# Range checks of a two-layer attention kernel: pieces of 128x256 in place of 128x512

## The chip, the core and the metric

The kernel runs on one core of a Trainium2 chip, which has 8 of them. A core has five engines that run side by side and wait for each other through semaphores: TensorE (PE, matrix products; its weight loads are listed as PEld), VectorE (DVE), ScalarE (ACT), GpSimd (POOL) and SyncE (SP), whose queue here issues most of the transfers. The engines work on a memory on the chip, SBUF, with 128 partitions; matmuls write to a second one, PSUM. A tile named 128x512 has 128 partitions and 512 float32 numbers in each.

The metric is the time of one execution on the device, in microseconds (us), the median of several runs. A profile is taken in a separate execution, in which every instruction is recorded; its time is a little different and is given beside its span.

## What is computed

An input of 128 x 256 x 256 (T, F, C) goes through two layers, each of which normalises by groups of channels (`_gn`), applies an attention along F for each of the 128 rows, and adds the result to its input. Layer 0 has 8 heads, a gate and an additive bias made from a second input `z`; layer 1 has 4 heads, and a query sees only keys at most 16 places away. Cut to what matters:

```python
# layer 0
scores = jnp.einsum('bsihc,bsjhc->bshij', q, k) * scale + b
mask2d = msa_mask[..., :, None] * msa_mask[..., None, :] > 0
scores = jnp.where(mask2d[:, :, None], scores, NEG_INF)
p = jax.nn.softmax(scores, axis=-1)
o = jnp.einsum('bshij,bsjhc->bsihc', p, v).reshape(B, s, i, h * c) * gate
x = x + (o @ Wo.T + bo)
# layer 1, on the result of layer 0
qkv = _gn(x).reshape(B * T, F, C) @ w_in.T + b_in
scores = jnp.einsum('bhid,bhjd->bhij', q, k) / jnp.sqrt(D)
scores = jnp.where(jnp.abs(i - j) <= band, scores, -jnp.inf)
attn = jax.nn.softmax(scores, axis=-1)
out = jnp.einsum('bhij,bhjd->bhid', attn, v)
x = x + (out @ w_out.T + b_out)
```

## The kernel before

The program holds two versions of the computation. `fast_kernel` leaves out what a softmax needs for extreme values (it takes exponentials without subtracting a maximum, and leaves out the mask), and checks as it goes that the numbers were in a range where this is right. `general_kernel` runs after it only where a check failed (`mixer_kernel`, L2067). With the inputs here it doesn't run.

A check is three VectorE instructions, in the helper `check` (L954 to 961): L958 compares the tile with a lower bound and writes 1 or 0 into a scratch tile `chk`; L959 compares with an upper bound and multiplies with `chk`; L960 takes the minimum along the row and writes it into one column of the tile `ok`. `chk` has one buffer of 128x512. At the end, L2060 takes the minimum over the columns of `ok`, and a small matmul brings the 128 rows together to the verdict.

Layer 1 works on pairs of rows: 64 pairs (`NP`), p = 0 to 63, in one loop from L1998. The order is written out by hand (`manual_schedule`), so every engine's instructions stand in the order in which the loop's lines issue them. An iteration finishes pair p-1 (`was`), does most of pair p (`now`) and prepares p+1, p+2 and p+3 (`nxt`, `nn`, `n3`). The parts that the prediction's steps touch, in the order of the loop:

- `now.scores(r)`: products of keys and queries (L1874, PE), their exponential (L1883, ACT), and the multiplication with the band's pattern `bw` (L1885, POOL, two instructions of 128x384).
- `was.apply(1)`: products with the values and the sums (L1903, PE).
- `nxt.product(n, i)`: seven products for queries (n = 0) and keys (n = 1) with the weights mixed in a fast scheme (L1824, PE), in the order 1, 2, 6, 5, 7, 4, 3. Each tile of PSUM is used twice over: `nxt.join(n, 2)` (L1835, VectorE) reads the result of product 2 and writes it into `qT` or `kT`, and product 5 then starts anew in the same PSUM tile. So product 5 waits for the join of product 2.
- `was.invert(1)`: the sums and their reciprocals (L1921, L1922, VectorE); `was.weigh(1)`: L1926, L1928 (VectorE).
- `was.out_row(r)`: the output projection (L1943, PE), and the addition of the input (L1947, VectorE).
- `nxt.values(r)`: L1860 (PE) and a copy (L1864, ACT).
- `nn.centre`, `nn.differences()`: L1786 (ACT), L1788 and L1795 to L1798 (POOL).
- `n3.turn()`: a transpose of 128x1024 on VectorE (L1781), one in each iteration up to p = 60.
- Then, as the last thing of an iteration with p > 0, one check from the list `checks`, if there is one (L2039). On VectorE it stands behind the transpose and ahead of the next iteration's joins for product 2.

The list `checks` is filled by `check_all` (L1964), one entry for each piece of 512 columns: the table `eb` (128x4096, 8 pieces), the mask (128x256, 1 piece), and the sums of layer 0 (`sums0`, 128x2048, 4 pieces). They go to iterations 1 to 13. In iteration 58, `load_sums` (L2004) fetches the sums of layer 1's first 56 pairs (`sums1`, 128x896) and adds pieces of 512 and 384 columns, which go to iterations 58 and 59. The last 8 pairs' reciprocals `rv` are checked directly in `weigh` (L1933, L1935), not through the list.

Of the kernel before, what the change touches and what calls it, by code (L numbers as in the profile page):

```python
# [9 lines left out]
F32 = mybir.dt.float32  # L10
# [6 lines left out]
P = 128  # L17
# [756 lines left out]
def fast_kernel(  # L774
# [41 lines left out]
    const = ctx.enter_context(tc.tile_pool(name="const", bufs=1))  # L816
# [114 lines left out]
    for a in range(KC):  # L931
        for h in range(H1):
            n = P // H1
# [5 lines left out]
    for h in range(H1):  # L939
        n = P // H1  # L940
# [7 lines left out]
    kb = const.tile([P, KC], F32, name="kb")  # L948
    vb_r = const.tile([P, C], F32, name="vb_r")
    bz_r = const.tile([P, H], F32, name="bz_r")  # L950
    ok = const.tile([P, 32], F32, name="ok")
    done = []

    def check(src, lo, hi, pool):  # L954

        n = src.shape[1]
        a = pool.tile([P, 512], F32, name="chk", tag="chk", bufs=1)[:, :n]
        nc.vector.tensor_scalar(a, src, lo, None, ALU.is_gt)  # L958
        nc.vector.scalar_tensor_tensor(a, src, hi, a, ALU.is_lt, ALU.mult)  # L959
        nc.vector.tensor_reduce(ok[:, len(done) : len(done) + 1], a, AX.X, ALU.min)  # L960
        done.append(src)
# [601 lines left out]
    behind, nx, n = None, 0, 0  # L1563
# [140 lines left out]
    with tc.tile_pool(name="l1", bufs=2) as sb, tc.tile_pool(  # L1704
        name="l1s", bufs=4
    ) as sm, tc.tile_pool(name="ps1_s", bufs=4, space=PSUM) as ps_s, tc.tile_pool(
        name="ps1_o", bufs=1, space=PSUM
# [254 lines left out]
        checks = []  # L1962

        def check_all(src, lo, hi):  # L1964
            for i in range(0, src.shape[1], 512):
                n = min(512, src.shape[1] - i)
                checks.append(lambda i=i, n=n: check(src[:, i : i + n], lo, hi, sm))

        def load_sums(src, name):
            t = sb.tile([P, src.shape[0] // P], F32, name=name, tag=name, bufs=1)  # L1970
            nc.sync.dma_start(t, src.rearrange("(a b) -> a b", a=P))
            check_all(t, 1e-16, 1e8)

        with tc.manual_schedule():
# [12 lines left out]
            for k in range(KC):  # L1987
                nxt.centre(k)
            nxt.differences()
        check_all(eb.rearrange("p h b i -> p (h b i)"), math.exp(-20.0), math.exp(20.0))  # L1990
        mask_t = sb.tile([S, I], F32, name="mask_all", bufs=1)
        nc.sync.dma_start(mask_t, mask)
        check_all(mask_t, 1e-15, 1e15)
        load_sums(rsum.rearrange("n q r c i -> (n q r c i)"), "sums0")

# [70 lines left out]
@with_exitstack  # L2066
def mixer_kernel(ctx, tc, *args):  # L2067

    nc = tc.nc
    keep = ctx.enter_context(tc.tile_pool(name="verdict", bufs=1))  # L2070
    verdict = keep.tile([1, 1], mybir.dt.int32, name="verdict")
    fast_kernel(tc, *args, verdict)
    again = nc.values_load(verdict[0:1, 0:1], min_val=0, max_val=1)
    with tc.If(again > 0):
        general_kernel(tc, *args)
# [53 lines left out]
```

## Time and profile before

| | us |
|---|---|
| median of 3 runs (3231.11 to 3235.41) | 3231.37 |
| the profiled execution | 3251.55 |
| its span, first to last instruction | 3249.8 |
| of it: layer 0 and what comes ahead of it (to about 2040) | 2040 |
| layer 1's beginning, to the transpose of its first iteration with a check | 83.4 |
| 13 intervals with a check of the list (2123.36 to 2362.70) | 239.3 |
| 42 intervals without a check (2362.70 to 3110.39) | 747.7 |
| the rest: pairs with checks of `rv` and `sums1`, and the end | 139.4 |

An interval is the time from one transpose (L1781) to the next, one iteration long. The page gives for each engine its busy time and its share of the span: PE 3073.5 us (95%), DVE 2339.4 (72%), POOL 2157.6 (66%), ACT 1537.5 (47%). These are means over stages that have different limits, so a change to one stage is read in that stage's own rows. In a timeline row stand the start, the length, the engine, the line, the operation, the tiles out<-in with their sizes, and in brackets how long the engine stood idle before it, with what ended the idling.

### The profile page before, as it was taken

To read this page: it belongs to the slowest core of one execution; us is meant where nothing else is said; L and a number is where in the kernel's file an instruction comes from. 1 tells how busy PE (TensorE), PEld (TensorE's weight loads), DVE (VectorE), ACT (ScalarE), POOL (GpSimd) and SP (SyncE) were. 2 spreads that over 40 slices of the span, in tenths; PEclk is the share of its full clock that TensorE was granted. 3 is DMA by queue.
4 is the path that set the end of the run, shared out by engine and by line. 5 is a ranking of instruction groups with operands and counts; after the bars stand their busy time and mean duration, and the time that the engine had idled before them with its cause. 6 is when DMAs were issued, how large, how long until landed. Compare 5 with 4: busy or idle time off the path is not lost.

```text
span 3249.8 us, 82756 instructions
## 1 busy us (share of the span) xinstructions
PE 3073.5 (95%) x34916; PEld 2066.9 (64%) x34916; DVE 2339.4 (72%) x3684; ACT 1537.5 (47%) x2501; POOL 2157.6 (66%) x1631
## 2 busy tenths in 40 slices
PE   5379999999999999999999999699999999999998
PEld 3245555555555555555555555488888888888886
DVE  7966676777777777777777777577766666666676
ACT  2255444444444444444444444255555555555553
POOL 3368888888888887888788886355454555545453
PEclk9799999999999999999999999899999999999999
DMA  9953333434433442344343332533334334343431
GB/s 349 391 150 63 65 88 86 95 70 96 95 95 70 95 91 64 87 92 95 70 95 96 67 88 70 106 80 89 92 88 92 91 90 95 85 100 86 94 93 47
DMA packets 726973, 329.10 MB, mean 101 GB/s; under 512 B 574560, under 2 KB 675808, under 8 KB 725440
## 3 DMA queue, kind: packets, MB, share of 16 engines
q1 hardware_dynamic: 721520, 320.81, 40.3%
q8 instruction: 277, 4.54, 0.7%
q10 hardware_dynamic: 5072, 2.90, 0.3%
q14 instruction: 104, 0.85, 0.1%
HBM read 254.88 MB, written 68.75 MB: 100 GB/s over the span
## 4 chain that ended last, share of the span: by engine, by line
PE 71%; DMA 12%; DVE 8%; POOL 4%; issue 2%; ACT 1%; SPq 1%; ACTq 0%; DVEq 0%; POOLq 0%
PE ps_p L1322 13%; PE ps_qk L1824 11%; PE ps_v L1860 7%; PE ps_su_y L1943 7%; PE ps_sc L1356 6%; PE ps_y L1443 5%; PE ps_ov L1388 5%; PE ps_v L1337 5%; PE ps_o L1903 3%; DMA rvb<-rsum 3%; PE ps_sc L1874 3%; DMA rs_d<-lrs 3%; DMA rsum<-rv 3%; PE ps_su L1396 2%; POOL eboth L1377 2%
## 5 line engine op out<-in xcount | busy, mean ns | idle before, releaser
L1377 POOL TENSOR_TENSOR eboth<-e 128x512 f32<-128x512 f32 x512 | 639.4, 1272 | 214.8 <-DVE e L1372 214.7
L1363 ACT ACTIVATE ps_sc<-ps_sc 128x1024 f32<-128x1024 f32 x512 | 492.8, 1006 | 575.9 <-PE ps_sc L1356 575.9
L1372 DVE TENSOR_TENSOR e<-ps_sc,eb 128x1024 f32<-128x1024 f32 x512 | 602.9, 1219 | 221.8 <-ACT ps_sc L1363 219.2
L1885 POOL TENSOR_TENSOR e<-e,bw 128x384 f32<-128x384 f32 x256 | 252.7, 1008 | 520.3 <-ACT e L1883 520.3
L1356 PE MATMUL ps_sc<-qT,kT 32*128 32x256 f32 x4096 | 293.3, 400 | 2.0 <-ACT kT L1326 2.0
L1443 PEld LDWEIGHTS ps_y<-wo,oT 128*128 128x128 f32 x1024 | 190.8, 190 | 106.6 <-POOL oT L1433 51.1
L1443 PE MATMUL ps_y<-wo,oT 128*128 128x256 f32 x1024 | 246.2, 383 | 12.8 <-POOL oT L1433 11.5
L1322 PE MATMUL ps_p<-xnT,wq 128*128 128x512 f32 x512 | 254.8, 619 | 2.6 <-POOL xnT L1309 2.3
L1309 POOL TENSOR_TENSOR xnT<-xgT,rs_r 128x512 f32<-128x512 f32 x128 | 160.1, 1273 | 135.4 <-DMA rs_r<-rs_d 133.2
L1943 PE MATMUL ps_su_y<-w_out,oT 128*128 128x256 f32 x1024 | 245.9, 384 | 3.8 <-DVE odd L1921 2.8
L1337 PE MATMUL ps_v<-wv,xnT 128*128 128x256 f32 x1024 | 248.6, 386 | 0.0
L1388 PE MATMUL ps_ov<-e,v 128*32 128x256 f32 x4096 | 247.7, 382 | 0.0
L1356 PEld LDWEIGHTS ps_sc<-qT,kT 32*128 32x128 f32 x4096 | 184.9, 184 | 94.4 <-issue 82.6
L1829 ACT ACTIVATE u<-ps_qk,bin_c 128x256 f32<-128x256 f32 x378 | 177.7, 478 | 141.2 <-PE ps_qk L1824 133.2
L1322 PE MATMUL ps_p<-xnT,wk 128*128 128x512 f32 x512 | 240.6, 592 | 0.0
L1860 PE MATMUL ps_v<-w_in,xgT 128*128 128x256 f32 x1024 | 238.3, 386 | 0.0
L1337 PEld LDWEIGHTS ps_v<-wv,xnT 128*128 128x128 f32 x1024 | 189.3, 190 | 76.8 <-issue 56.9
L1322 PE MATMUL ps_p<-xgT,wg 128*128 128x512 f32 x512 | 236.8, 605 | 0.0
L1922 DVE RECIPROCAL rv<-odd 128x256 f32<-128x256 f32 x128 | 224.4, 1753 | 4.4
L1943 PEld LDWEIGHTS ps_su_y<-w_out,oT 128*128 128x128 f32 x1024 | 196.4, 192 | 32.3 <-DVE odd L1921 3.6
L1860 PEld LDWEIGHTS ps_v<-w_in,xgT 128*128 128x128 f32 x1024 | 189.3, 190 | 32.8 <-issue 0.5
L1824 PE MATMUL ps_qk<-dT,wst 128*128 128x256 f32 x756 | 191.4, 389 | 5.2 <-DVE qT L1835 5.1
(198 smaller groups left out, 5694.3 us busy)
## 6 DMA issues: line engine op xcount, KB each, us to landing
xa<-in_x_dram SPq DMA_DIRECT2D x8, 4096.0 KB
xt<-in_x_dram SPq DMA_DIRECT2D x64, 512.0 KB
x<-xo SPq DMA_DIRECT2D x16, 2048.0 KB
xs<-x SPq DMA_DIRECT2D x256, 128.0 KB
xt<-x SPq DMA_DIRECT2D x64, 512.0 KB
xs<-in_x_dram SPq DMA_DIRECT2D x252, 128.0 KB
rvb<-rsum SPq DMA_DIRECT2D x252, 128.0 KB
out_dram<-yo SPq DMA_DIRECT2D x63, 512.0 KB
```

What stands on the lines that cost most here:

```text
L1322: nc.tensor.matmul(ps, w[:, k, m * P : (m + 1) * P], getattr(self, src)[:, k, :], start=(k == 0), stop=(k == KC - 1),)
L1337: nc.tensor.matmul(self.ps_v[:, b * C : (b + 1) * C], self.xnT[:, k, t * P : (t + 1) * P], wv[:, k, :], start=(k == 0), stop=(k == KC - 1),)
L1356: nc.tensor.matmul(self.pss[q // 2][:, q % 2, b, :], self.kT[rs, c, r * I + b * P : r * I + (b + 1) * P], self.qT[rs, c, r * I : (r + 1) * I],
L1363: nc.scalar.activation(self.pss[a], self.pss[a], AF.Exp)
L1372: nc.vector.tensor_tensor(e, pss[a], eb[:, h : h + 2], ALU.mult)
L1377: nc.gpsimd.tensor_tensor(t, es[a][:, :, 0, :], es[a][:, :, 1, :], ALU.add)
L1388: nc.tensor.matmul(ov[q * D0 : (q + 1) * D0, c, :], self.v[:, r, b, h * D0 : (h + 1) * D0], es[q // 2][:, q % 2, b, :], start=(b == 0), st ...
L1443: nc.tensor.matmul(self.ps_y[:, b * C : (b + 1) * C], self.oT[r][:, k, b * P : (b + 1) * P], wo[:, k, :], start=(k == 0), stop=(k == KC - 1),)
L1824: nc.tensor.matmul(to, lhs, rhs, start=start, stop=True, skip_group_check=True)
L1860: nc.tensor.matmul(ps[:, b * C : (b + 1) * C], self.xgT[:, k, t * P : (t + 1) * P], w_in[:, k, 2 * C : 3 * C], start=(k == 0), stop=(k == ...
L1885: nc.gpsimd.tensor_tensor(e[:, q], e[:, q], bcast(bw.rearrange("p b w -> p (b w)"), 1, KC), ALU.mult)
L1943: nc.tensor.matmul(ps[:, b], self.oT[r][:, k, b * P : (b + 1) * P], w_out[:, k, :], start=(k == 0), stop=(k == KC - 1),)
```

## The change

`check_all` cuts its tiles into pieces of 256 columns in place of 512. Each piece is an entry of `checks` of its own, so one iteration checks at most 256 columns, and the list lasts longer: `eb` 16 pieces, the mask 1, `sums0` 8 (iterations 1 to 25), and `sums1` 256, 256, 256 and 128 columns (iterations 58 to 61). The checks in `weigh` keep their size. The tile `ok` gets 48 columns in place of 32, since 38 are now used in place of 24.

```diff
@@ -948,7 +948,7 @@
-    ok = const.tile([P, 32], F32, name="ok")
+    ok = const.tile([P, 48], F32, name="ok")
@@ -1962,8 +1962,8 @@
         def check_all(src, lo, hi):
-            for i in range(0, src.shape[1], 512):
-                n = min(512, src.shape[1] - i)
+            for i in range(0, src.shape[1], 256):
+                n = min(256, src.shape[1] - i)
                 checks.append(lambda i=i, n=n: check(src[:, i : i + n], lo, hi, sm))
```

## The prediction

> **What bounds the kernel now.** I read the page's totals first (TensorE busy 95% of the span), then went straight to layer 1's loop, the only place that the diff touches, and read it in four views. First the waits over 2123.36 to 2362.70 us, which hold 13 pairs, each with one range check:
>
> ```profile
> PEld ps_qk L1824 <- DVE qT L1835: 9.5, 12, 0.8
> PE ps_qk L1824 <- DVE qT L1835: 4.7, 12, 0.4
> ```
>
> TensorE waits for the vector engine 12 times in 13 pairs; in the next 13 pairs (2362.70 to 2602.00), which have no check, the same view has neither line. Which pair goes free is the question. The table by stretches answers it, one pair to a row, from one transpose at L1781 to the next:
>
> ```profile
> 2252.59:2271.06 18.47, 18.08 (x327) 14.77 (x316) 14.73 (x21) 9.40 (x20) 9.63 (x10) 1.00 0.42 87
> 2271.06:2288.86 17.80, 17.80 (x326) 14.79 (x316) 14.06 (x21) 9.40 (x20) 9.48 (x10) 1.00 0.39 92
> 2288.86:2307.32 18.46, 18.07 (x326) 14.77 (x316) 14.72 (x21) 9.41 (x20) 9.62 (x10) 1.00 0.38 87
> 2362.70:2380.50 17.80, 17.80 (x326) 14.85 (x316) 11.98 (x18) 9.41 (x20) 9.44 (x10) 1.00 0.42 91
> ```
>
> Columns: stretch and length, busy PE, PEld, DVE, ACT, POOL, granted clock, DMA share, GB/s. The rows are a pair with 128x512 of eb checked, the pair with mask_all (128x256), one with 128x512 of the sums, and one with no check. The mask's pair is as short as the unchecked one, and PE is busy throughout both. So the kernel of before already contains one check of the new size, in the place where the new ones will stand.
>
> Third, the tile chk, for durations (min/median/max ns):
>
> ```profile
> L958 DVE TENSOR_SCALAR chk<-rv x9: 284/420/421, 3118.8 to 3236.9; 128x512 f32<-128x512 f32 x7, 128x256 f32<-128x256 f32 x2
> L959 DVE SCALAR_TENSOR_TENSOR chk<-rv,chk x9: 424/691/693, 3119.3 to 3237.2; 128x512 f32<-128x512 f32 x7, 128x256 f32<-128x256 f32 x2
> L958 DVE TENSOR_SCALAR chk<-eb x8: 1199/1204/1208, 2124.5 to 2253.8; 128x512 f32<-128x512 f32 x8
> L959 DVE SCALAR_TENSOR_TENSOR chk<-eb,chk x8: 1372/1374/1377, 2125.8 to 2255.0; 128x512 f32<-128x512 f32 x8
> L958 DVE TENSOR_SCALAR chk<-mask_all x1: 1066/1066/1066, 2272.2 to 2272.2; 128x256 f32<-128x256 f32 x1
> L959 DVE SCALAR_TENSOR_TENSOR chk<-mask_all,chk x1: 1103/1103/1103, 2273.3 to 2273.3; 128x256 f32<-128x256 f32 x1
> ```
>
> The checks of rv, which meet no GpSimd work, take 420 and 691 ns at 512 wide. Those after the transpose take 1204 and 1374, nearly as much at 256: most of it is waiting. Fourth, the timeline of a 512 pair and of the mask's, the moment where it is decided:
>
> ```profile
> 2142.90 2.14 POOL L1885 TENSOR_TENSOR e<-e,bw 128x384 f32<-128x384 f32 x2
> 2145.05 1.26 PE L1824 MATMUL ps_qk<-dT,wst 128*128 128x256 f32 x4
> 2146.23 0.42 DVE L1835 TENSOR_TENSOR qT<-ps_qk,u 128x256 f32<-128x256 f32 x1
> 2146.70 1.99 PE L1824 MATMUL ps_qk<-dT,wst 128*128 128x256 f32 x8 [0.39 <-DVE qT L1835]
> ...
> 2272.14 2.00 POOL L1885 TENSOR_TENSOR e<-e,bw 128x384 f32<-128x384 f32 x2
> 2274.29 2.98 PE L1824 MATMUL ps_qk<-dT,wst 128*128 128x256 f32 x12
> 2274.46 0.42 DVE L960 TENSOR_REDUCE ok<-chk 128x1 f32<-128x256 f32 x1
> 2274.79 0.41 DVE L1835 TENSOR_TENSOR qT<-ps_qk,u 128x256 f32<-128x256 f32 x1
> ```
>
> With 512 the join (L1835) comes 4.41 us after its pair's transpose and PE breaks off after 4 matmuls (the two products with number 6) until the join for qT has freed the PSUM bank of the next product, number 5; with 256 it comes at 3.73 us and PE's 12 matmuls run through.
>
> **What the skill says.** "SBUF — State Buffer", "Who interferes with whom": a VectorE operation in a 2-port mode (a tensor_scalar can be), or with two SBUF inputs while GpSimd reads SBUF, fully blocks until the GpSimd operation that was first ends; a tensor_reduce never contends. The trace agrees: L958 and L959 stretch, L960 is 686 or 687 ns in both places, and L959 ends 0.55 us after L1885 (2145.59 against 2145.04). "VectorE: DVE Perf Modes", on the TRN2 errata: a fixed cost per instruction, so tile at 512 elements or more; its formula gives (512+151)/0.96 = 691 ns and (256+151)/0.96 = 424, as the rv rows have. By that page halving is wasteful; it speaks of VectorE's time, which here is not the bound in a pair without a check.
>
> **The change, part by part.** The instruction order of both programs differs in the checks alone, by 14 more of them (42 VectorE instructions); PE, ACT, POOL and SP keep theirs.
>
> Removed: 8 pairs with 512 of eb. From 2123.36 to 2271.06 they took 147.70 us; 8 unchecked pairs take 8 x 17.80 = 142.42 (17.802 is the mean over 2362.70 to 3110.39, 42 pairs). Gain 5.28. The 4 pairs with sums0, 2288.86 to 2362.70: 73.84 - 71.21 = 2.63. sums1: its 512 piece's pair took 18.66 and its 384 piece's 18.32. Beside them stand checks of rv; the pair behind them, by the values' products at L1860 (3177.50 to 3195.50), has the rv check alone and takes 18.00. Gain 0.66 + 0.32 = 0.98. Sum 8.89 us.
>
> Put in: 16 pieces of eb, 1 of the mask as before, 8 of sums0, at pairs 1 to 25 in a row, then 256, 256, 256 and 128 columns of sums1 at pairs 58 to 61. The chain in one: L1885's end sets when L959 can stream, and behind that come 0.27 us of L959 in place of 0.55 and 0.42 of L960 in place of 0.69; with 0.13 from a shorter L958, which lets go of L1885's second half sooner, this is the 0.68 by which the join is earlier. Cost on the path, as in the mask's pair: 0.00, hidden beside PE's products number 6, with next to nothing to spare. That shows in the 384 piece: its three operations are 0.34 us longer than the mask's (1134+1243+553 ns against 1066+1103+420) and its pair 0.32 longer. So the slope is one and the corner lies at 256 columns. I take 0.00 for each of the 28; bounds -0.01 (the rounding of 17.80) and +0.10 (if the corner lies a little elsewhere without the profiler, see below). Of the additional 12 main pairs, what is queued behind the check is the join, the reciprocal (L1922) and the next joins; in the mask's pair they have caught up by the last join, 9.70 us after the transpose against 9.71 unchecked, so nothing is carried into the next pair. At pairs 60 and 61 the checks are new: at 60 as elsewhere, at 61 there is no transpose and VectorE stands idle 2.98 us before its join. Cost 0.
>
> The wider ok (24 to 38 columns in the last reduction, 169 ns before, by an estimate of 14/0.96 = 15 ns longer) sits under VectorE's 3.79 us of idling before its last row sum. It also moves most later tiles by 64 bytes; no row shows what that does, and I take 0 with -1 to +1.
>
> Sum: -8.9 us. On the profiled execution: 3251.6 - 8.9 = 3242.7. The runs' median is 20 us (0.6%) lower; the pairs can be at most that much shorter there, which moves the gain by 0.05. So 3231.4 - 8.9 = 3222.5 us, -0.28%.
>
> **Rivals.** (A) The corner. If each 256 check leaves a rest, 28 x 0.10 = 2.8 comes back: 3225.3; at 0.15 the gain is under 6.5 us, that is, within 0.2%. For it: the corner is tight and the executions without a profile are faster. Against: the mask's pair, at rounding. (B) Slower: the blocked time. If twelve or more consecutive pairs with checks push GpSimd's L1885 back, L959 ends later in each and the join with it. It decides from 8.9/28 = 0.32 us per check; were a 256 check as dear as a 512 one (0.66), the sum is 28 x 0.66 - 8.9 = +9.6: 3241. For it: L958 and L959 are 1066 and 1103 ns at 256, nearly those of 512. Against: L1885 starts 1.08 us after the transpose in checked and unchecked pairs alike (1.09). (C) The gain is eaten elsewhere, no change, 3231: another engine or DMA paces the loop. Against it: 42 unchecked pairs at 17.80 with PE busy throughout and the clock at 1.00 in every row.
>
> **How the numbers follow.** Forecast 83%, A to within 0.2% 9%, C 3%, B 5%. About 0.2%, 6.5 us, is what a measurement here can tell from no change; the forecast clears it by 2.4 us, and three runs of before spread by 4.3, so I move 3 of its 83 points to "same". Faster 0.80, same 0.15, slower 0.05. Range: 28 x 0.10 and 1 above, with 2 to 3 for the runs: 3229; below, 1 for the shifted tiles, with 2 to 3 for the runs: 3218.5.
>
> **What would show it.** Right: 25 intervals of 17.80 between transposes from the first check on, L958 near 1066 and L959 near 1103 ns on eb, no waits of ps_qk for qT. Wrong: intervals above 17.9 with such waits, or time gained there that shows up in layer 0 or at the end.

## The result, and the profile after

The changed kernel takes 3221.72 us (median of 8 runs, 3220.38 to 3228.63), the kernel before in the same measurement 3231.78 (8 runs, 3229.77 to 3237.17). The ratio is 0.997, with a 95% interval from 0.9961 to 0.9979, that is, 6.8 to 12.6 us faster.

The table by stretches of the kernel after, columns as before (length, busy PE, PEld, DVE, ACT, POOL, clock, DMA): the first iteration with a piece of eb, one with eb in the middle, the last with sums0, and the two behind it from iterations 58 and 59, in which a piece of sums1 stands beside a check of rv.

```profile
2102.84:2120.64 17.80, 17.80 (x327) 14.78 (x316) 14.06 (x21) 9.42 (x20) 9.49 (x10) 1.00 0.38 92
2209.66:2227.46 17.80, 17.80 (x325) 14.77 (x316) 14.07 (x22) 9.42 (x20) 9.49 (x10) 1.00 0.40 93
2530.09:2547.89 17.80, 17.80 (x326) 14.78 (x316) 14.05 (x21) 9.42 (x20) 9.48 (x10) 1.00 0.40 91
3118.75:3136.74 17.99, 17.99 (x326) 14.95 (x316) 15.66 (x24) 9.42 (x20) 9.48 (x10) 1.00 0.38 89
3136.74:3154.74 18.00, 18.00 (x327) 14.96 (x316) 15.67 (x24) 9.42 (x20) 9.49 (x10) 1.00 0.39 91
```

PE is busy for the whole of each stretch. The 25 intervals with a piece of the list, 2102.84 to 2547.89, take 445.05 us, which is 25 x 17.80. In the kernel before, iterations 1 to 25 took 239.34 (13 with a check) and 12 x 17.80 = 213.6 (without): 452.9. Iterations 58 and 59 took 36.98 and take 35.99. So 7.9 and 1.0, together 8.9 us, are gone where the checks are.

The waits over these 25 iterations, all that name ps_qk (who waited for whom, us in total, times, longest):

```profile
ACT u L1829 <- PE ps_qk L1824: 49.6, 75, 1.0
ACT qT L1831 <- PE ps_qk L1824: 42.1, 25, 1.7
ACT kT L1831 <- PE ps_qk L1824: 9.7, 25, 0.4
PEld ps_qk L1824 <- ACT u L1829: 9.2, 25, 0.4
DVE kT L1835 <- PE ps_qk L1824: 6.0, 25, 0.2
```

The view lists no wait of TensorE for the join at L1835 any more. The timeline of one interval shows how close it is; the first line is GpSimd's, the next four VectorE's, the last TensorE's:

```profile
2210.74 2.00 POOL L1885 TENSOR_TENSOR e<-e,bw 128x384 f32<-128x384 f32 x2
...
2210.81 1.08 DVE L958 TENSOR_SCALAR chk<-eb 128x256 f32<-128x256 f32 x1
2211.93 1.10 DVE L959 SCALAR_TENSOR_TENSOR chk<-eb,chk 128x256 f32<-128x256 f32 x1
2213.06 0.42 DVE L960 TENSOR_REDUCE ok<-chk 128x1 f32<-128x256 f32 x1
2213.40 0.41 DVE L1835 TENSOR_TENSOR qT<-ps_qk,u 128x256 f32<-128x256 f32 x1
...
2212.88 2.98 PE L1824 MATMUL ps_qk<-dT,wst 128*128 128x256 f32 x12
```

The join for qT starts 3.74 us after the interval's beginning, and the 12 matmuls run through. L959 ends 0.28 us after GpSimd's L1885 in each of the 25 intervals.

The weight loads show where the limit lies. First the load for product 5 and its matmul in the kernel before, in the 512 interval that the prediction shows, then both here:

```profile
2146.70 0.30 PEld L1824 LDWEIGHTS ps_qk<-dT,wst 128*128 128x128 f32 x2 [0.79 <-DVE qT L1835]
2146.70 0.48 PE L1824 MATMUL ps_qk<-dT,wst 128*128 128x256 f32 x1 [0.39 <-DVE qT L1835]
```

```profile
2213.87 0.30 PEld L1824 LDWEIGHTS ps_qk<-dT,wst 128*128 128x128 f32 x2
2213.98 0.38 PE L1824 MATMUL ps_qk<-dT,wst 128*128 128x256 f32 x1
```

In both, the load starts 0.05 us after the end of qT's join (at 2146.65 and at 2213.82). So the load still waits for the join at 256 columns, though the view of waits doesn't list it. Only the matmul behind it no longer does: it starts 0.11 to 0.12 us after its load in the 25 intervals, and together with it in the 512 interval. A matmul that starts together with its load is followed by the next one after 0.32 us, the others here after 0.22, so by this estimate a load needs a lead of 0.10 us, and 0.01 to 0.02 us is left.

The two profiled executions differ by more than the medians: 3251.55 us before, which is above all 8 runs of the kernel before, and 3220.51 after, spans 3249.8 and 3218.8. Of these 31.0 us, 20.5 lie ahead of the first interval with a check (it begins at 2123.36 and at 2102.84), where the change does nothing. In layer 0 (500 to 2000 us), GpSimd waited for the transfer into rs_r 112.2 us in the one and 42.4 us in the other profile. Whether that belongs to the change was left to the experiments. The rest is 8.9 for the checks, 2.2 at the very end, from the last transpose on (66.2 and 64.1 us), less 0.6 lost in the interval ahead of iteration 58. The 2.2 isn't the change's either: e8_after, with the same program, takes 65.6 there, and e1_ok48, with the pieces of before, 65.8. In the kernel before, the last eight matmuls of L1943 took 3.78 us at a granted clock of 0.51; in the first profile of the changed kernel they took 1.99 at 1.00.

### The profile page after: what moved, and what is told of

Read it like the earlier page. It is cut to its first block, busy times and chain, and to the rows that moved or that the text cites. A ratio compares the mean times of both kernels' runs of the same rounds, so it can differ in the third digit from the quotient of the medians.

```text
span 3218.8 us, 82798 instructions
## 1 busy us (share of the span) xinstructions
PE 3056.0 (95%) x34916; PEld 2066.4 (64%) x34916; DVE 2345.1 (73%) x3726; ACT 1538.2 (48%) x2501; POOL 2159.2 (67%) x1631
## 4 chain that ended last, share of the span: by engine, by line
PE 91%; DVE 4%; DMA 3%; ACT 1%; issue 0%; POOL 0%; SPq 0%; ACTq 0%; POOLq 0%; DVEq 0%
PE ps_p L1322 21%; PE ps_qk L1824 13%; PE ps_sc L1356 8%; PE ps_v L1860 7%; PE ps_ov L1388 7%; PE ps_v L1337 7%; PE ps_su_y L1943 7%; PE ps_y L1443 7%; PE ps_o L1903 4%; PE ps_su L1396 3%; PE ps_sc L1874 3%; DVE st L1178 2%; DMA xa<-in_x_dram 2%; PE ps_su_y L1903 2%; DVE zst L1103 1%; DMA zt<-in_z_dram 1%
## 5 line engine op out<-in xcount | busy, mean ns | idle before, releaser
L1885 POOL TENSOR_TENSOR e<-e,bw 128x384 f32<-128x384 f32 x256 | 252.1, 1007 | 512.2 <-ACT e L1883 512.2
L1943 PE MATMUL ps_su_y<-w_out,oT 128*128 128x256 f32 x1024 | 243.6, 381 | 4.3 <-DVE odd L1921 2.8
L1922 DVE RECIPROCAL rv<-odd 128x256 f32<-128x256 f32 x128 | 224.4, 1753 | 4.4
L1943 PEld LDWEIGHTS ps_su_y<-w_out,oT 128*128 128x128 f32 x1024 | 195.0, 191 | 32.2 <-DVE odd L1921 3.5
L1343 DVE TENSOR_TENSOR v<-ps_v,vb_r 128x512 f32<-128x512 f32 x128 | 88.5, 691 | 149.3 <-PE ps_v L1337 149.2
```

The lines of the kernel that those rows point to most:

```text
L1885: nc.gpsimd.tensor_tensor(e[:, q], e[:, q], bcast(bw.rearrange("p b w -> p (b w)"), 1, KC), ALU.mult)
L1943: nc.tensor.matmul(ps[:, b], self.oT[r][:, k, b * P : (b + 1) * P], w_out[:, k, :], start=(k == 0), stop=(k == KC - 1),)
```

## The experiments

They ran on three chips on which the kernel before takes 3283 us (3282.6 to 3284.1), some 52 us more than in the measurement above. Times are therefore compared only through the ratio to the kernel before on the same chip.

**e1_ok48: the wider ok alone**

```diff
-    ok = const.tile([P, 32], F32, name="ok")
+    ok = const.tile([P, 48], F32, name="ok")
```

> The kernel before, with the tile ok 48 columns wide in place of 32 and the pieces left at 512: the later tiles move by 64 bytes, nothing else changes. Theory (the gain is the checks' alone, in layer 1): no change to before within 2 us, checked intervals 18.46 us, unchecked 17.80. Rival (the moved addresses gave part of the gain, for instance through layer 0's transfers, where the profile of before had 112 us of GpSimd waiting for rs_r and that of after 42): faster than before by several us with the intervals unchanged.

Measured: 3282.39 us, before 3283.29, ratio 0.9998 (0.9989 to 1.0007). Intervals with a piece of 512 of eb or sums0: 18.45 to 18.47. GpSimd waited for rs_r 139.1 us in layer 0, more than in either profile above. No part of the gain is seen here: the intervals keep their length, and the ratio leaves room for 3.6 us at most.

**e2_384 and e7_320: other sizes of the pieces**

```diff
-            for i in range(0, src.shape[1], 256):
-                n = min(256, src.shape[1] - i)
+            for i in range(0, src.shape[1], 384):
+                n = min(384, src.shape[1] - i)
```

(320 in the other; both differences are to the changed kernel.)

> Pieces of 384 columns. Theory (slope one from a corner at 256 columns): intervals with a 384 piece 18.13 us, 17 such pieces, so 5.6 us slower than the changed kernel and some 3.3 us faster than before. Rival (the fixed cost of each instruction decides, so fewer pieces are better): not slower than the changed kernel, or interval at 17.80.

> Pieces of 320 columns. Theory (slope one from a corner at 256): intervals with a 320 piece 17.96 us, half of what 384 adds. Rival (a step between 320 and 384): 17.80.

One interval of each by stretches, 384 and then 320:

```profile
2175.74:2193.87 18.13, 18.07 (x326) 14.76 (x316) 14.40 (x22) 9.43 (x20) 9.55 (x10) 1.00 0.39 90
```

```profile
2172.82:2190.79 17.97, 17.97 (x326) 14.76 (x316) 14.24 (x22) 9.40 (x20) 9.54 (x10) 1.00 0.39 91
```

All 15 intervals with a 384 piece are 18.12 to 18.14 us, all 18 with a 320 piece 17.95 to 17.97. With 17.80 at 256 and 18.46 at 512 the four sizes lie on a line: 0.16 or 0.17 us for each 64 columns above 256. Its terms can be read from the timelines: L959 ends 0.28, 0.35, 0.41 and 0.55 us after GpSimd's L1885 at 256, 320, 384 and 512 columns, and the join starts 0.34, 0.40, 0.47 and 0.60 us after L960. The other 0.13 us between 256 and 512 are L1885's own, which ends later at 512. In the 10 intervals with 384 columns of eb, the waits show the join again:

```profile
PEld ps_qk L1824 <- DVE qT L1835: 4.6, 10, 0.5
```

That is 0.46 us each, 0.13 more than the interval loses, as at 512 (0.79 and 0.66). At 256 columns PEld is idle ahead of the load for just these 0.13 us (2213.74 to 2213.87), and nothing is lost.

Time with 384: 3278.19 us, ratio 0.9986 (0.9979 to 0.9992), so 5.1 us faster than before by the medians where 3.3 was expected; 3.3 of 3283 is a ratio of 0.9990, within the interval. The changed kernel's gain was about double. e7_320 has a single run, whose total can't be told from others; its intervals can.

**e3_two256: two pieces of 256 in each iteration**

```diff
-                if checks and p > 0:
-                    checks.pop(0)()
+                for _ in range(2):
+                    if checks and p > 0:
+                        checks.pop(0)()
```

> Pieces of 256 columns, two of them in each iteration, one directly behind the other: as many columns for each iteration as before, in six instructions. Theory (what counts is when the join behind the checks can start; the second piece meets no GpSimd work and starts its three instructions in 0.32, 0.46 and 0.34 us): intervals 17.80 + 1.12 = 18.92 us, 12 of them and two at the end, so 15.7 us slower than the changed kernel and 6.8 us slower than before. Rival (the number of columns for each iteration decides): intervals of 18.46, as before.

VectorE's timeline of one iteration:

```profile
2157.75 1.08 DVE L958 TENSOR_SCALAR chk<-eb 128x256 f32<-128x256 f32 x1
2158.86 1.10 DVE L959 SCALAR_TENSOR_TENSOR chk<-eb,chk 128x256 f32<-128x256 f32 x1
2160.00 0.42 DVE L960 TENSOR_REDUCE ok<-chk 128x1 f32<-128x256 f32 x1
2160.46 0.29 DVE L958 TENSOR_SCALAR chk<-eb 128x256 f32<-128x256 f32 x1
2160.79 0.43 DVE L959 SCALAR_TENSOR_TENSOR chk<-eb,chk 128x256 f32<-128x256 f32 x1
2161.25 0.42 DVE L960 TENSOR_REDUCE ok<-chk 128x1 f32<-128x256 f32 x1
2161.58 0.41 DVE L1835 TENSOR_TENSOR qT<-ps_qk,u 128x256 f32<-128x256 f32 x1
```

The first piece waits for GpSimd, the second doesn't (0.29 and 0.43 us in place of 1.08 and 1.10). Intervals are 19.03 to 19.05 us, not 18.46: the same columns for each iteration as before cost more, since they come in six instructions. The expected 18.92 missed 0.12. It is in the step from the first L960 to the second L958: 0.46 us from start to start, where the L1835 that follows the other L960 starts after 0.33. The second L958 writes the tile `chk` that L960 reads (there is one buffer), and L1835 touches nothing of L960's. In this trace an instruction of VectorE that uses a tile of the one before it, and finds nothing else to wait for, starts 0.03 us after that one's listed end (L959 behind L958, L960 behind L959, L1922 behind L1921); one that uses none starts some 0.08 us before it. The second L958 is of the first kind. That the one buffer makes it so is argued from these rows; no run had two. Time: 3293.08 us, ratio 1.0031 (1.0020 to 1.0043), slower than before by 9.8 (6.8 expected, a ratio of 1.0021, inside the interval).

**e4_gap512: pieces of 512 in an idle place**

```diff
                 now.apply(0)
+                if checks and 0 < p < NP - LATE:
+                    checks.pop(0)()
                 now.combine(0)
...
-                if checks and p > 0:
+                if checks and p > NP - LATE:
                     checks.pop(0)()
```

(The difference is to the kernel before.)

> Pieces of 512 columns as before, but in the 13 main iterations the check stands in another place: ahead of the sums' addition and reciprocal of the iteration's own pair (L1921, in combine(0)), where VectorE is idle for 2.09 us and GpSimd is idle until the second L1885. The two pieces of sums1 stay where they were. Theory (the place and GpSimd's hold on the shared port make a 512 piece dear, not its size): L958 0.42 us and L959 near 0.69, intervals 17.80, so 7.9 us faster than before and within 1.5 us of the changed kernel. Rival (a pair has room on VectorE for 256 columns of checks and no more): intervals near 18.46, no faster than before.

The groups of the tile chk for eb (durations min/median/max in ns), and the place in VectorE's timeline, with GpSimd's next work in the last line:

```profile
L958 DVE TENSOR_SCALAR chk<-eb x8: 416/417/419, 2150.3 to 2274.9; 128x512 f32<-128x512 f32 x8
L959 DVE SCALAR_TENSOR_TENSOR chk<-eb,chk x8: 691/691/693, 2150.8 to 2275.4; 128x512 f32<-128x512 f32 x8
```

```profile
2203.37 0.42 DVE L1835 TENSOR_TENSOR kT<-ps_qk,u 128x256 f32<-128x256 f32 x1 [0.27 <-PE ps_qk L1824]
2203.71 0.42 DVE L958 TENSOR_SCALAR chk<-eb 128x512 f32<-128x512 f32 x1
2204.16 0.69 DVE L959 SCALAR_TENSOR_TENSOR chk<-eb,chk 128x512 f32<-128x512 f32 x1
2204.89 0.69 DVE L960 TENSOR_REDUCE ok<-chk 128x1 f32<-128x512 f32 x1
2205.89 0.42 DVE L1921 TENSOR_TENSOR odd<-ps_su_y,odd 128x256 f32<-128x256 f32 x1 [0.31 <-ACT odd L1916]
...
2204.83 1.95 POOL L1885 TENSOR_TENSOR e<-e,bw 128x384 f32<-128x384 f32 x2 [8.13 <-ACT e L1883]
```

GpSimd has been idle for 8.13 us until L959 is at its end. Here the same two instructions take 417 and 691 ns in place of 1204 and 1374, and 0.31 us of idling is left behind the check. All 13 intervals are 17.79 or 17.80 us. Time: 3272.44 us, ratio 0.9966 (0.9954 to 0.9978). So a piece of 512 is not too big for an iteration; it was too long in one place. The new place differs in two things: GpSimd is idle, which the durations show, and no instruction that TensorE waits for stands close behind. The run doesn't separate the two. By an estimate from these rows the first is enough: in the old place a check of 512 as short as this one would let the join start 2.94 us after the transpose (1.16 to L958, as in the kernel before, and 1.78 for the check), earlier than the 3.73 of the mask's pair.

**e5_none and e10_none: no checks from the list**

```diff
-                checks.append(lambda i=i, n=n: check(src[:, i : i + n], lo, hi, sm))
+                pass
```

> The changed kernel with the list of checks left empty: the checks of eb, of the mask and of both tables of sums are left out, those of rv stay. Theory (a 256 piece costs nothing on the path): the intervals that lose a check stay at 17.80 us and the time is that of the changed kernel within 1 us. Rival A (each 256 piece leaves a rest of 0.05 to 0.15 us): 1.4 to 4.2 us faster than the changed kernel.

> The kernel with the list of checks left empty once more (the checks of eb, the mask and both tables of sums are left out), beside the changed kernel on the same chip. Theory: within 1 us of the changed kernel. Rival A (a rest of 0.05 to 0.15 us for each piece): 1.4 to 4.2 us faster than it.

Measured: 3274.51 us, ratio 0.9971 (0.9959 to 0.9983), and on another chip 3272.61, ratio 0.9973 (0.9962 to 0.9984), beside 3273.24 for the changed kernel there: 0.6 us under it. All of the 25 intervals that lost their only check are 17.80 or 17.81. The 28 pieces of 256 or less together cost nothing that these runs can show; the totals alone, with some 4 us to each side, would not settle it.

**e8_after: the changed kernel on another chip**

> The changed kernel once more, on a chip on which the kernel before takes some 52 us longer, to stand beside the next two on one chip. Theory: layer 1's intervals as in its first profile, 17.80 us, and 9 us (7 to 12) faster than before, since what makes such a chip slower lies ahead of layer 1. Rival (the gain of the first measurement came partly from layer 0): another difference, with the same intervals.

Measured: 3273.24 us, before 3282.62, ratio 0.9966 (0.9954 to 0.9979), 9.4 us faster; 25 intervals of 17.80 or 17.81 again. GpSimd's waits for rs_r in layer 0 are 141.7 us here, with the very program that showed 42.4 in its first profile, so this wait belongs to the execution or the chip and not to the change.

**e6_late and e9_late: the last checks of rv in idle places**

```diff
+        held = []
+        def release():
+            while held:
+                held.pop(0)()
...
-                    check(rv.rearrange("p r i -> p (r i)"), 1e-16, 1e8, sm)
+                    held.append(lambda: check(rv.rearrange("p r i -> p (r i)"), 1e-16, 1e8, sm))
                 elif self.p == NP - 1:
-                    check(rv[:, r, :], 1e-16, 1e8, sm)
+                    held.append(lambda: check(rv[:, r, :], 1e-16, 1e8, sm))
...
                 now.apply(0)
+                release()
                 now.combine(0)
...
             now.apply(0)
+            release()
             now.combine(0)
             was.out_row(1)
             now.apply(1)
+            release()
             now.combine(1)
             now.out_row(0)
+            release()
             now.out_row(1)
```

> The changed kernel, with the checks of rv in the last 8 pairs taken out of weigh and put into places where VectorE is idle: ahead of the iteration's own combine(0), ahead of the two last combines, and ahead of the very last addition L1947. Theory (these checks stand on the path: 0.20 us in each of 6 iterations, and 1.78, 1.12 and 1.12 us ahead of the last row sums): intervals of 18.00 become 17.80 and the time is 3 to 5 us under the changed kernel. Rival (the reciprocals' checks are hidden, or their new places are on the path as much): within 1 us of the changed kernel.

> The kernel with the checks of rv in idle places once more, beside the changed kernel on the same chip. Theory: 3 to 5 us faster than the changed kernel. Rival: within 1 us of it.

The end of the first of them on VectorE (lines of the code moved by nine, so okmin is L2069 here):

```profile
3256.37 0.68 DVE L1947 TENSOR_TENSOR yo<-ps_su_y,xt 128x512 f32<-128x512 f32 x1
3256.97 0.28 DVE L958 TENSOR_SCALAR chk<-rv 128x256 f32<-128x256 f32 x1
3257.29 0.43 DVE L959 SCALAR_TENSOR_TENSOR chk<-rv,chk 128x256 f32<-128x256 f32 x1
3257.75 0.42 DVE L960 TENSOR_REDUCE ok<-chk 128x1 f32<-128x256 f32 x1
3258.20 0.19 DVE L2069 TENSOR_REDUCE okmin<-ok 128x1 f32<-128x38 f32 x1
3259.14 0.69 DVE L1947 TENSOR_TENSOR yo<-ps_su_y,xt 128x512 f32<-128x512 f32 x1 [0.74 <-PE ps_su_y L1943]
```

The check now stands between the two last additions, where VectorE waits for TensorE. The intervals of 18.00 become 17.80, also those with both a piece of sums1 and a check of rv. Times: 3269.93 us, ratio 0.9962 (0.9949 to 0.9976), and 3266.52, ratio 0.9956 (0.9944 to 0.9968), 6.7 us under the changed kernel's median on that chip, where 3 to 5 was expected. From the last transpose to the end of the span it is 61.4 us in both profiles, 64.1 and 65.6 in the changed kernel's two. A part of this is the clock, which the expectation didn't have: of the last two groups of eight matmuls of L1943, one ran at 0.54 to 0.58 in the changed kernel's profiles (3.30 us in one, 3.61 in the other), and both ran at 1.00 (1.99 us each) in these two. Whether moving the checks keeps the clock up was not tried. By the medians this version is the fastest; its interval overlaps that of the changed kernel, so its lead is not certain.

## Why the prediction was right

- *The wait that goes.* The prediction had TensorE stand still for the join at L1835 in 12 of 13 pairs, and took the mask's pair to show the new size without this wait. The 25 pairs of the kernel after repeat the mask's to 0.01 us, and sizes of 320 and 384 bring the loss back in proportion. (Its stretch of 13 pairs without a check, 239.3 us, holds 13.4 of them; the reading is the same.)
- *The terms.* The prediction had eb at 5.28, sums0 at 2.63 and sums1 at 0.98, in sum 8.89. The profile shows 7.9 for the first two and 1.0 for the third. The medians moved by 10.1 and, on another chip, by 9.4; with intervals of some 3 and 4 us to each side, they don't tell 8.9 from these.
- *The 28 new pieces at nothing.* The 25 intervals are 17.80 with the pieces and without them, so rival A, a rest of 0.05 to 0.15 for each piece, falls by the profiles. The medians of e10_none and e8_after agree (0.6 us) but are too coarse to exclude the smaller rests.
- *The corner.* It lies at 256 columns, as taken from the 384 piece of sums1, and "next to nothing to spare" was 0.01 to 0.02 us by the estimate above. That a check of 256 fits at all is the luck of this kernel's sizes; the prediction knew that it does from the mask's pair. Its worry that executions without a profile are faster rested on 3251.55 against 3231.37; with 3220.51 for the changed kernel's profile, below its median, the profile isn't what made that difference.
- *GpSimd's hold on the port.* In the prediction this rested on the Trainium skill's page "SBUF — State Buffer", "Who interferes with whom", and on rows of different tiles. e4_gap512 shows the stretching on the same tile and size: 417 and 691 ns away from L1885, 1204 and 1374 beside it. That it is a port which GpSimd holds is the page's word; the traces agree, in that L959 ends a fixed time after L1885 for each size (0.28 us at 256 columns, 0.55 at 512). What the prediction gave for the page's word that a tensor_reduce never contends, L960 at 686 in both places, showed nothing, since GpSimd had ended L1885 before L960 began (2145.04 and 2145.63). In e4_gap512 L960 does run beside L1885 and takes 0.69 us, which agrees with the page. Rival B falls with the 25 intervals in a row.
- *The 64 bytes.* 0 with -1 to +1 was taken; e1_ok48 gives 0.9998 (0.9989 to 1.0007), which is 0.9 us less, within 3.6 less to 2.3 more. That agrees, but doesn't show the bound of 1.
- *The loop's pace.* Rival C falls: nothing else took the gain back.

What the prediction missed is in the profiled execution: 3242.7 was worked out for it and 3220.5 came. The step "on the profiled execution" took layer 0 to be equal in both, and layer 0 differed by 20 us from one execution to the next. The forecast for the median didn't depend on it, since it was made as a difference.

## What to carry to other kernels

Where a kernel repeats one loop body, compare the length of one round with and without the extra work: rounds that happen to have a smaller piece give the price of a smaller piece, before anything is changed. Work on an engine that isn't the bound costs only what it delays the next instruction that the bound waits for, so its place and the size of one portion count and not its sum: by the intervals' rows, two pieces of 256 keep VectorE busy for 4.2 us (2 x 14.06 - 2 x 11.98) where one of 512 kept it for 2.7 (14.73 - 11.98), and the kernel became faster. When a small operation takes much longer than elsewhere, look at what else holds what it needs at that moment; the same check cost nothing at twice the size in a place where GpSimd was idle.

## What was not expected

- Two checks in a row cost 1.24 us for the second, not 1.12: its first instruction writes the tile that L960 before it reads, and starts 0.46 us after L960's start in place of 0.33.
- The same program differs by 52 us (1.6%) between the first measurement and e8_after, and the difference is ahead of layer 1's loop: its first transpose starts at 2042 us in the changed kernel's first profile and at 2097 in e8_after's, while the 25 intervals agree to 0.01 us. GpSimd's waits for rs_r go with it (42.4 and 141.7 us; the profile of the kernel before lies between, with 2064 and 112.2). That they are its cause was not shown.
- The interval ahead of iteration 58's transpose, in which the sums of layer 1 are fetched, varies without a pattern in the change: 18.22 us before, 18.81 after, 18.09 to 18.79 in the experiments. In the changed kernel's first profile TensorE stands still there for 0.49 us, with no other engine named. Its cause was not tried.
